# Deformable-attention bias network: four sets of 32 outputs on pairs of keys, in place of two sets of 64 on single keys

## The chip, the cores and the metric

The kernel runs on one core of one Trainium2 chip, in float32 throughout. The metric is the device time of one execution in microseconds; lower is better. A core has TensorE for matmuls (PE; its weight loads are shown apart as PEld), VectorE (DVE), ScalarE (ACT), GpSimd (POOL) and SyncE (SP), which mostly starts transfers.

## The reference, cut to what matters

Four layers follow each other: a deformable attention block with an MLP, then three smaller attention-like blocks. Only the attention of the first is touched. It has 2 batches and 8 heads of 64 channels; 1024 queries (32 x 32 pixels) look at 64 sampled keys per head. Beside the usual q·k score each (query, key) has a bias from a small network on their relative position:

```
pos  = grid_q[:, :, None, :] - grid_kv[:, None, :, :]        # 2 numbers per (query, key)
bias = sign(pos) * log1p(abs(pos))
bias = relu(bias @ cpb_w1 + cpb_b1)                          # 2 -> 128
bias = relu(bias @ cpb_w2 + cpb_b2)                          # 128 -> 128
bias = bias @ cpb_w3 + cpb_b3                                # 128 -> 1
sim  = einsum('bhid,bhjd->bhij', qh, kh) + bias
out  = softmax(sim) @ v
```

That is 2 x 8 x 64 x 1024, about a million (query, key) pairs, each through a 128 x 128 layer. The signs of `cpb_w3` decide how outputs of the second layer can be added before the third: |w3| is multiplied into the second layer's weights (a relu lets a positive factor through), so the third layer is a sum with signs +1 and -1.

## The kernel before, in words

A step treats one key of two heads (512 steps n, in 8 groups g of 64; a group is a batch and a pair of heads).

- `first(n)` (line 334): VectorE adds an x part and a y part out of a small table, with a relu: two instructions (heads) of 128 x 1024 into `h1`, 128 hidden units on the partitions. Three `h1` buffers; it runs two keys ahead.
- `second(n, o)` (line 553), o = 0 and 1: TensorE, four column tiles of 32 side by side, eight matmuls of 512 columns (each shows as two records), into PSUM tile `ph`; ScalarE evicts it with bias and relu into `r0` or `r1`. Each `r` tile has 64 hidden units of the one half of the pixels and 64 of the other on its partitions. `ph` has two buffers.
- `combine(n)` (line 571): VectorE computes r0 += rel * r1, where `rel` is the ratio of signs of the two halves, so that the third layer has a contraction over 64 for each half of the pixels.
- `third(g, i)` (line 592): on four keys, TensorE multiplies the combined tiles by a window of the sign columns `cw3` and adds into the score tile `psim`, which `scores(g)` (line 575) started with q·k. The score tile's 128 rows mix 64 keys and the two halves of the pixels.
- `attend(g, ...)` (line 714): eviction of `psim`, transposes (`flip`), maximum (`top`), `sub`, `exp`, `total`, `norm`, transposes back (`back`), spread as small pieces over the next group's steps. `prepare(g)` (line 609) computes the sampled keys and values of a coming group, spread in the same way. A convolution's taps on VectorE (`chain`, line 830) and the tables' scaling on ScalarE are spread too.

The spreading is written out by hand: `at(n, when, fn)` files a piece of work under a step and a half-step, and `run(n, when)` emits it there. `pin` keeps each engine's instructions of this part in the program's order. So an engine's order is the order in which the loop calls the functions:

```
for n in range(NK):
    second(n, 0);  run(n, 0)
    second(n, 1);  first(n + 2);  combine(n - 1);  run(n, 1)
```

Ahead of that loop stands a lead-in (lines 352 to 532): loads, normalization, queries, transposes of x and the offset convolution of the first group, with small instructions that make `sgn`, `rel`, `b2a`, `cw3` and the weights `w2a`. Behind it stand the output projection, the MLP and the other three layers.

Of the kernel before, what the change touches and what calls it, by code (L numbers as in the profile page):

```python
# [10 lines left out]
F32 = mybir.dt.float32  # L11
# [25 lines left out]
    ("L0_conv_cpb_w1", 2), ("L0_conv_cpb_b1", 1), ("L0_conv_cpb_b2", 2), ("L0_conv_cpb_w3", 2),  # L37
# [27 lines left out]
def conv_seq(  # L65
# [60 lines left out]
    with ExitStack() as ctx_l0:  # L126
# [3 lines left out]
        kblk = l0.tile([P, 2, 2, P], F32, name="kblk")  # L130
# [195 lines left out]
        w2a = l0.tile([P, P], F32, name="w2a")  # L326
        sgn = l0.tile([P, 2], F32, name="sgn")
        b2a = l0.tile([P, 2], F32, name="b2a")
        cw3 = l0.tile([P, 47], F32, name="cw3")
        rel = l0.tile([P, 1], F32, name="rel")  # L330
        h1p = ctx_att.enter_context(tc.tile_pool(name="h1p", bufs=3))
# [20 lines left out]
        with tc.tile_pool(name="a", bufs=1) as a, tc.tile_pool(name="aps", bufs=3, space=PSUM) as aps, tc.tile_pool(  # L352
# [75 lines left out]
            pin(nc.vector.tensor_scalar(sgn, v("L0_conv_cpb_w3"), 0.0, 2.0, ALU.is_ge, ALU.mult))  # L428
            pin(nc.vector.tensor_scalar(sgn, sgn, -1.0, None, ALU.add))
            pin(nc.vector.memset(cw3, 0.0))  # L430
            pin(nc.vector.tensor_copy(cw3[0:DH, 15:16], sgn[0:DH, 0:1]))
            pin(nc.vector.tensor_copy(cw3[DH:P, 31:32], sgn[DH:P, 0:1]))
            pin(nc.vector.tensor_tensor(rel, sgn[:, 0:1], sgn[:, 1:2], ALU.mult))
            pin(nc.vector.tensor_tensor(b2a, v("L0_conv_cpb_w3"), sgn, ALU.mult))
            pin(nc.vector.tensor_tensor(b2a, b2a, v("L0_conv_cpb_b2"), ALU.mult))
# [77 lines left out]
            pin(nc.scalar.activation(w2a, cpbw[:, P : 2 * P], AF.Abs))  # L513
            pin(nc.vector.tensor_tensor(w2a, w2a, cpbw[:, 0:P], ALU.mult))
# [23 lines left out]
        with tc.tile_pool(name="hid", bufs=3) as hid, tc.tile_pool(name="sm", bufs=1) as sm, tc.tile_pool(name="hps", bufs=2, space=PSUM) as hps, tc.tile_pool(  # L538
# [3 lines left out]
            r0s, r1s, psims = {}, {}, {}  # L542
# [10 lines left out]
            def second(n, o):  # L553
                ph = hps.tile([P, 2, 512], F32, name="ph")
                for h in range(2):
                    for t in range(4):
                        half, s = divmod(t, 2)
                        pin(
                            nc.tensor.matmul(  # L559
                                ph[t * 32 : (t + 1) * 32, h, :],  # L560
                                lhsT=w2a[:, o * DH + s * 32 : o * DH + (s + 1) * 32],
                                rhs=h1s[n][:, h, half * 512 : (half + 1) * 512],
                                start=True,
                                stop=True,
                            )
                        )
                r = hid.tile([P, 2, 512], F32, name=f"r{o}", bufs=(7, 3)[o])
                pin(nc.scalar.activation(r, ph, AF.Relu, bias=b2a[:, o : o + 1]))  # L568
                (r0s, r1s)[o][n] = r

            def combine(n):
                r0, r1 = (r.rearrange("p h n -> p (h n)") for r in (r0s[n], r1s.pop(n)))
                pin(nc.vector.scalar_tensor_tensor(r0, r1, rel, r0, ALU.mult, ALU.add))  # L573

            def scores(g):
                k, b = divmod(g, B)
                ps = psims[g] = sps.tile([P, 2, 512], F32, name="psim")
                for half in range(2):
                    for h in range(2):
                        hs = slice(h * DH, (h + 1) * DH)  # L580
                        pin(
                            nc.tensor.matmul(  # L582
                                ps[:, h, :],
                                lhsT=kblk[hs, g % 2, half, :],
                                rhs=q[hs, k, b * HW + half * 512 : b * HW + (half + 1) * 512],
                                start=(half == 0),
                                stop=False,
                                skip_group_check=True,
                            )
                        )  # L590

            def third(g, i):
                n = g * J + 4 * i
                for h in range(2):
                    for m in range(4):
                        pin(
                            nc.tensor.matmul(  # L597
                                psims[g][m * 32 : (m + 1) * 32, h, :],
                                lhsT=cw3[:, 15 - i : 47 - i],
                                rhs=r0s[n + m][:, h, :],  # L600
                                start=False,
                                stop=(i == 15),
                                skip_group_check=True,
                            )
                        )
                for m in range(4):
                    del r0s[n + m]

            def prepare(g):
# [53 lines left out]
                def keys():  # L663

                    for half in range(2):
                        pin(
                            nc.vector.tensor_scalar(
                                kblk[:, g % 2, half, :].rearrange("p (m s i) -> p m s i", m=4, s=2)[:, :, half, :],
                                st["pk"][:, 0, :].rearrange("p (m i) -> p m i", m=4),
                                DH**-0.5,  # L670
                                None,
                                ALU.mult,
                            )
                        )

                def values():
                    for h in range(2):
                        hs = slice(h * DH, (h + 1) * DH)
                        pin(nc.vector.tensor_copy(vblk[hs, g % 2, h, :], st["pk"][hs, 1, :]))
# [34 lines left out]
            def attend(g, n, step):  # L714
# [4 lines left out]
                def evict(h):  # L719
                    if h == 0:  # L720
# [3 lines left out]
                            st["simt"][:, h, :], psims[g][:, h, :], AF.Identity, bias=v("L0_conv_cpb_b3")  # L724
# [3 lines left out]
                def flip(h):  # L728

                    pt = st["pt", h] = mps.tile([P, 4, 2, 4, 16], F32, name="psm", tag="m")  # L730
                    for t in range(4):
                        pin(
                            nc.tensor.transpose(
                                pt[:, t].rearrange("p s m i -> p m s i"), st["simt"][:, h, t * P : (t + 1) * P], ident
# [3 lines left out]
                def top(h):  # L738
                    if h == 0:
                        st["mx"] = sm.tile([P, 2, 8], F32, name="mx")  # L740
                        st["e"] = sm.tile([P, 2, 4, 2, J], F32, name="e")
                        st["den"] = sm.tile([P, 2, 8], F32, name="den")
                    pt = st["pt", h].rearrange("p t s m i -> p (t s) (m i)")
                    pin(nc.vector.tensor_reduce(st["mx"][:, h, :], pt, AX.X, ALU.max))

                def sub(h):
                    pt = st["pt", h].rearrange("p t s m i -> p t s (m i)")
                    mx = st["mx"][:, h, :].rearrange("p (t s) -> p t s", s=2)
                    pin(
                        nc.vector.tensor_tensor(  # L750
                            st["e"][:, :, :, h, :].rearrange("p s t j -> p t s j"),
                            pt,
                            mx.unsqueeze(3).to_broadcast([P, 4, 2, J]),
# [4 lines left out]
                def ef(s):  # L758
                    return st["e"][:, s].rearrange("p t h j -> p (t h) j")

                def exp(s, half):
                    es = ef(s)[:, half * 4 : half * 4 + 4, :]
                    pin(nc.scalar.activation(es, es, AF.Exp))

                def total(s):
                    pin(nc.vector.tensor_reduce(st["den"][:, s, :], ef(s), AX.X, ALU.add))

                def norm(s):
                    den = st["den"]
                    if s == 0:  # L770
                        pin(nc.vector.reciprocal(den, den))
                    pin(
                        nc.vector.tensor_tensor(
                            ef(s), ef(s), den[:, s, :].unsqueeze(2).to_broadcast([P, 8, J]), ALU.mult
                        )
                    )

                def back(s):
                    pb = st["pb", s] = mps.tile([P, 512], F32, name="pb", tag="m")
                    for t in range(4):  # L780
# [3 lines left out]
                                st["e"][:, s, t].rearrange("p h j -> p (h j)"),  # L784
# [4 lines left out]
                def keep_(s):  # L789
# [5 lines left out]
                    (2, 1, top, 0), (4, 1, sub, 0), (6, 1, top, 1), (8, 1, sub, 1),  # L795
                    (10, 0, exp, 0, 0), (11, 0, exp, 0, 1), (12, 0, exp, 1, 0), (13, 0, exp, 1, 1),
# [25 lines left out]
            for g in range(NG):  # L822
                prepare(g)
                at(J * g + 5, 1, scores, g)
                for i in range(16):
                    at(J * g + 4 * i + 5, 1, third, g, i)
                if g < NG - 1:
                    attend(g, J * (g + 1) + 2, True)
# [24 lines left out]
            for n in range(NK):  # L853
                second(n, 0)
                run(n, 0)
                second(n, 1)
                if n + 2 < NK:
                    first(n + 2)
                if n:
                    combine(n - 1)  # L860
                h1s.pop(n)
                run(n, 1)
            combine(NK - 1)
# [674 lines left out]
def _layout(a):  # L1538
# [12 lines left out]
    for name, (at, w) in _AT.items():  # L1551
# [7 lines left out]
        elif name in ("L0_conv_cpb_b2", "L0_conv_cpb_w3"):  # L1559
            x = np.tile(x.reshape(2, DH).T, (2, 1))  # L1560
# [83 lines left out]
```

## Time and profile before

| what | us |
|---|---|
| median of 3 runs (2898.55 to 2899.06) | 2899.02 |
| the profiled execution | 2898.92 |
| its span, first to last instruction | 2897.1 |
| first second layer starts | 45.8 |
| last third layer ends | 2096.4 |
| busy in the span: PE, DVE, ACT, POOL | 2848.6, 2281.3, 1510.7, 2.0 |

A group's line in the profile names the line of the kernel, the engine and the operation, the tile written and those read, the shape, the count, then busy time and mean duration in ns, then idle time of that engine just before the instructions, and what ended most of that idle time. A timeline's line gives start, duration, engine, line, operation and count. Four matmuls on neighbouring column tiles run side by side, so their durations overlap, and it is the distance between starts that says what they cost.

### The profile page before, as it was taken

Reading aid. Unit: us, or ns where it says so; the run is one execution under the profiler, and the core shown is the slowest. Engines: PE = TensorE matmul, PEld = TensorE weight load, DVE = VectorE, ACT = ScalarE, POOL = GpSimd, SP = SyncE. Lnnn points to the kernel's source line nnn. Section 1 sums busy time; section 2 is a strip of 40 time slices with the busy share of each in tenths; the row PEclk is TensorE's granted clock in tenths of the full one; section 3 lists DMA queues with packets and bytes.
Section 4 is the critical chain, followed back from the end, with each engine's and each line's share of the span. In section 5 each row is a group of like instructions: output and inputs, shape, how many; then the busy total and the mean of one; then the engine's idle time right before and its main releaser. Section 6 shows DMA issues by size and latency. Waiting matters only on the chain.

```text
span 2897.1 us, 48614 instructions
## 1 busy us (share of the span) xinstructions
PE 2848.6 (98%) x21304; PEld 1018.9 (35%) x21304; DVE 2281.3 (79%) x2486; ACT 1510.7 (52%) x1759; POOL 2.0 (0%) x8
## 2 busy tenths in 40 slices
PE   8999999999999999999999999999999999999996
PEld 4233233333333333333333333333344444455453
DVE  6999899999999989998998998898764454523545
ACT  6666666667666666666666666666512111110244
POOL 0000000000000000000000000000000000000000
PEclk9999999999999999999999999999999999999998
DMA  3000000000000000000010001000010000010001
GB/s 113 16 16 16 17 30 16 16 16 16 16 16 26 22 16 16 16 16 16 16 41 34 16 16 45 16 16 16 14 38 15 22 29 22 1 73 1 0 1 58
DMA packets 21971, 66.41 MB, mean 23 GB/s; under 512 B 1504, under 2 KB 10848, under 8 KB 17024
## 3 DMA queue, kind: packets, MB, share of 16 engines
q1 hardware_dynamic: 21328, 62.79, 6.0%
q8 instruction: 168, 2.75, 0.4%
q10 hardware_dynamic: 432, 0.52, 0.1%
q14 instruction: 43, 0.35, 0.0%
HBM read 58.84 MB, written 4.46 MB: 22 GB/s over the span
## 4 chain that ended last, share of the span: by engine, by line
PE 96%; ACT 2%; DVE 1%; DMA 0%; issue 0%; ACTq 0%; DVEq 0%; SPq 0%
PE ph L559 61%; PE psim L597 8%; PE A L1017 4%; PE D L1017 4%; PE C L1017 4%; PE pr L1264 2%; PE B L1017 2%; PE po L952 2%; PE pg L1160 1%; PE pa L1255 1%; PE pz L1366 1%; PE pu L1194 1%; PE pscore L1337 1%; PE psim L582 1%; PE pr L1377 1%; PE pf L1304 0%
## 5 line engine op out<-in xcount | busy, mean ns | idle before, releaser
L559 PE MATMUL ph<-h,w2a 128*32 128x512 f32 x16384 | 1790.4, 593 | 1.6 <-ACT r L568 1.6
L568 ACT ACTIVATE r<-ph,b2a 128x1024 f32<-128x1024 f32 x1024 | 1142.7, 1116 | 730.5 <-PE ph L559 713.2
L339 DVE CUSTOM_DVE_ANT_1 h<-tab 128x1024 f32<-128x1024 f32 x1024 | 1205.5, 1218 | 157.5 <-PE ph L559 157.2
L559 PEld LDWEIGHTS ph<-h,w2a 128*32 128x32 f32 x16384 | 524.1, 109 | 1215.4 <-issue 842.4
L573 DVE SCALAR_TENSOR_TENSOR r<-r,rel,r 128x1024 f32<-128x1024 f32 x512 | 654.2, 1278 | 7.0 <-ACT r L568 7.0
L597 PE MATMUL psim<-r,cw 128*32 128x512 f32 x2048 | 244.4, 593 | 0.0
L163 ACT ACTIVATE tab<-tab,vec 128x256 f32<-128x256 f32 x252 | 137.3, 545 | 0.0
L597 PEld LDWEIGHTS psim<-r,cw 128*32 128x32 f32 x2048 | 65.8, 110 | 155.3 <-issue 154.2
L1057 ACT COPY u<-A 128x512 f32<-128x512 f32 x16 | 9.4, 586 | 146.8 <-PE A L1017 146.8
L1036 ACT ACTIVATE h<-h,vec 128x512 f32<-128x512 f32 x32 | 23.1, 721 | 113.6 <-DVE h L1039 113.6
L1017 PE MATMUL A<-xn,w 128*128 128x512 f32 x128 | 60.3, 593 | 0.8 <-DVE x L959 0.8
L1017 PE MATMUL C<-hT,w 128*128 128x512 f32 x128 | 60.3, 592 | 0.0
L1039 DVE TENSOR_TENSOR h<-C,u 128x512 f32<-128x512 f32 x32 | 22.1, 691 | 48.3 <-PE C L1017 48.0
L1017 PE MATMUL A<-h,w 128*128 128x512 f32 x128 | 60.1, 592 | 0.0
L952 PE MATMUL po<-q,vwo 128*128 128x512 f32 x128 | 56.1, 594 | 0.4 <-ACT r L568 0.4
L1264 PE MATMUL pr<-x,A 128*128 128x512 f32 x128 | 55.1, 592 | 0.0
L220 DVE SCALAR_TENSOR_TENSOR acc<-q,vec,acc 128x128 f32<-128x128 f32 (+3 forms) x88 | 46.3, 526 | 0.8
L1077 DVE TENSOR_TENSOR x<-D,x 128x512 f32<-128x512 f32 x32 | 22.1, 691 | 26.0 <-PE D L1017 26.0
L1077 DVE TENSOR_TENSOR x<-C,x 128x512 f32<-128x512 f32 x32 | 22.1, 691 | 24.8 <-PE C L1017 24.8
L1160 PE MATMUL pg<-xt 128*128 128x512 f32 (+3 forms) x128 | 36.4, 439 | 0.8 <-ACT xt L1158 0.6
L1017 PEld LDWEIGHTS A<-xn,w 128*128 128x128 f32 x128 | 24.2, 190 | 31.8 <-issue 30.1
L1017 PEld LDWEIGHTS A<-h,w 128*128 128x128 f32 x128 | 24.3, 190 | 30.6 <-issue 30.1
(269 smaller groups left out, 1644.0 us busy)
## 6 DMA issues: line engine op xcount, KB each, us to landing
tab<-fd SPq DMA_DIRECT2D x31, 1024.0 KB, 4.6
lw<-in_l_w_dram SPq DMA_DIRECT2D x5, 1024.0 KB
x<-in_x_dram SPq DMA_DIRECT2D x4, 1024.0 KB, 5.4
w<-in_mlp_w_dram SPq DMA_DIRECT2D x8, 512.0 KB, 3.9
w<-in_mlp_w_dram SPq DMA_DIRECT2D x16, 256.0 KB, 3.0
out_dram<-r SPq DMA_DIRECT2D x8, 512.0 KB, 2.7
xn<-in_x_dram SPq DMA_DIRECT2D x3, 1024.0 KB
xn<-in_x_dram SPq DMA_DIRECT2D x4, 256.0 KB, 5.6
```

The source lines that it names most:

```text
L163: return nc.scalar.activation(tf, tf if src is None else src[:, :, :, ax, :], AF.Identity, bias=0.0 if ax == 0 else v("L0_conv_cpb_b1"), s ...
L220: pin(nc.vector.scalar_tensor_tensor(dst, src, wt_, dst, ALU.mult, ALU.add))
L339: nc.vector._custom_dve(TENSOR_ADD_SAT, out=h1[:, h], in0=tab[:, j, h, 0, :].unsqueeze(1).to_broadcast([P, 32, 32]), in1=tab[:, j, h, 1, : ...
L559: nc.tensor.matmul(ph[t * 32 : (t + 1) * 32, h, :], lhsT=w2a[:, o * DH + s * 32 : o * DH + (s + 1) * 32], rhs=h1s[n][:, h, half * 512 : (h ...
L568: pin(nc.scalar.activation(r, ph, AF.Relu, bias=b2a[:, o : o + 1]))
L573: pin(nc.vector.scalar_tensor_tensor(r0, r1, rel, r0, ALU.mult, ALU.add))
L597: nc.tensor.matmul(psims[g][m * 32 : (m + 1) * 32, h, :], lhsT=cw3[:, 15 - i : 47 - i], rhs=r0s[n + m][:, h, :], start=False, stop=(i == 1 ...
L952: nc.tensor.matmul(po, lhsT=vwo[:, k * B + t // 2, o * P : (o + 1) * P], rhs=q[:, k, ts_], start=(k == 0), stop=(k == KC - 1),)
L1017: nc.tensor.matmul(banks[bank], lhsT=a[an][k], rhs=b_[bn_][k], start=(i < 4 and k == 0), stop=(k == n - 1), skip_group_check=True,)
L1077: nc.vector.tensor_tensor(to, t, to, ALU.add)
L1160: nc.tensor.matmul(pgs[i], lhsT=xt[:, i * P : (i + 1) * P], rhs=xt[:, i * P :], start=(t == 0), stop=(t == 7),)
L1264: nc.tensor.matmul(pr, lhsT=A[b][:, k, o * P : (o + 1) * P], rhs=x[:, k, ns], start=(k == 0), stop=(k == KC - 1),)
```

## The change

The second layer's 128 outputs are made in four sets of 32. For one set, the four column tiles hold two heads by two halves of the pixels, so a `ph` tile [...] holds one set of *two* keys. Four such sets (o = 0 to 3) of a pair of keys p are evicted to `r0` to `r3`; then

- r0 += rel0 * r1 and r2 += rel1 * r3 on VectorE (`combine(p, 0)`, `combine(p, 2)`);
- r0 += r2 by a transfer that adds (`join(p)`), issued from GpSimd's queue.

For the last addition to need no factor, the outputs are ordered so that sets 0 and 2 have the same sign in each row: `order` makes that order from the signs of `cpb_w3`, by small GpSimd operations on masks, for the biases and signs and again for the 128 x 128 weights. The third layer's contraction of 128 now covers two heads and two halves of the pixels at once; a third on four keys has one matmul per key in place of two.

The score tile becomes two tiles [...], 32 keys and four (head, half) blocks of rows. `scores` uses all 128 rows of the contraction, with keys laid out in blocks (`kblk` twice as large; filled by four ScalarE instructions in place of two on VectorE). `attend` follows: a maximum over each of two key blocks and one small maximum of the two, `sub` behind both. Pieces move by one or two steps: scores to (64g + 6, 0), thirds to (64g + 4u + 6, 1), attend by two keys. `h1` gets four buffers; `r0` to `r3` get 4, 1, 2 and 1, each for a pair of keys.

```diff
-            def second(n, o):
+            def second(p, o):
                 ph = hps.tile([P, 2, 512], F32, name="ph")
-                for h in range(2):
+                for i in range(2):
                     for t in range(4):
-                        half, s = divmod(t, 2)
+                        half, h = divmod(t, 2)
                         pin(
                             nc.tensor.matmul(
-                                ph[t * 32 : (t + 1) * 32, h, :],
-                                lhsT=w2a[:, o * DH + s * 32 : o * DH + (s + 1) * 32],
-                                rhs=h1s[n][:, h, half * 512 : (half + 1) * 512],
+                                ph[t * 32 : (t + 1) * 32, i, :],
+                                lhsT=w2a[:, o],
+                                rhs=h1s[2 * p + i][:, h, half * 512 : (half + 1) * 512],
...
-                r = hid.tile([P, 2, 512], F32, name=f"r{o}", bufs=(7, 3)[o])
-                pin(nc.scalar.activation(r, ph, AF.Relu, bias=b2a[:, o : o + 1]))
+                r = hid.tile([P, 2, 512], F32, name=f"r{o}", bufs=(4, 1, 2, 1)[o])
+                pin(nc.scalar.activation(r, ph, AF.Relu, bias=sb3[:, o, 1:2]))
...
+            def combine(p, o):
+                r0, r1 = (r.rearrange("p i n -> p (i n)") for r in (rs[p, o], rs.pop((p, o + 1))))
+                i = o // 2
+                pin(nc.vector.scalar_tensor_tensor(r0, r1, rel[:, i : i + 1], r0, ALU.mult, ALU.add))
+
+            def join(p):
+                nc.gpsimd.dma_start(rs[p, 0], rs.pop((p, 2)), accum_op=ALU.add)
...
-            def third(g, i):
-                n = g * J + 4 * i
-                for h in range(2):
-                    for m in range(4):
-                        pin(
-                            nc.tensor.matmul(
-                                psims[g][m * 32 : (m + 1) * 32, h, :],
+            def third(g, u):
+                kb, i = divmod(u, 8)
+                p = (g * J + 4 * u) // 2
+                for m in range(4):
+                    pin(
+                        nc.tensor.matmul(
+                            psims[g, kb][m * 32 : (m + 1) * 32, :],
+                            lhsT=cw3[:, 7 - i : 39 - i],
+                            rhs=rs[p + m // 2, 0][:, m % 2, :],
...
-            for n in range(NK):
-                second(n, 0)
-                run(n, 0)
-                second(n, 1)
-                if n + 2 < NK:
-                    first(n + 2)
-                if n:
-                    combine(n - 1)
-                h1s.pop(n)
-                run(n, 1)
-            combine(NK - 1)
+            for p in range(NK // 2):
+                for o in range(4):
+                    n = 2 * p + o // 2
+                    second(p, o)
+                    if o == 0 and p:
+                        combine(p - 1, 2)
+                        join(p - 1)
+                    elif o == 2:
+                        combine(p, 0)
+                    elif n + 2 < NK and o % 2:
+                        first(n + 2)
+                    run(n, o % 2)
+                for i in range(2):
+                    h1s.pop(2 * p + i)
+            combine(NK // 2 - 1, 2)
+            join(NK // 2 - 1)
```

The new function that orders the outputs, and its calls in the lead-in:

```diff
+        def order(to, of, w3, pool):
+            n = w3.shape[2]
+            gp = nc.gpsimd
+            m = pool(9 * n).rearrange("p (i n) -> p i n", n=n)
+            g, same, swap, other, keep_ = (m[:, 0:4], m[:, 4], m[:, 5], m[:, 6], m[:, 7])
+            tmp, nswap = m[:, 8], m[:, 0]
+            pin(nc.vector.tensor_scalar(g, w3, 0.0, None, ALU.is_ge))
+            for d, k in ((same, 2), (swap, 1)):
+                gp.tensor_tensor(d, g[:, 0], g[:, k], ALU.subtract)
+                gp.tensor_tensor(d, d, d, ALU.mult)
...
+            mix(0, (0, keep_), (1, other))
+            mix(1, (1, same), (2, swap), (0, other))
+            mix(2, (2, nswap), (1, swap))
+            gp.tensor_copy(to[:, 3], of[:, 3])
...
-            pin(nc.vector.tensor_tensor(rel, sgn[:, 0:1], sgn[:, 1:2], ALU.mult))
-            pin(nc.vector.tensor_tensor(b2a, v("L0_conv_cpb_w3"), sgn, ALU.mult))
...
+            order(sb3, wb, w3, part)
...
+            w2r = part(P)
+            w3r = cpbw[:, P : 2 * P]
+            pin(nc.scalar.activation(w2r, w3r, AF.Abs))
+            nc.gpsimd.tensor_tensor(w2r, w2r, cpbw[:, 0:P], ALU.mult)
+            order(w2a, w2r.rearrange("p (s o) -> p s o", s=4), w3r.rearrange("p (s o) -> p s o", s=4), part)
```

## The prediction

> **What bounds the kernel now.** I read the page's busy shares first, then the costliest groups, then the busy times of the stretch that the change rewrites, then its timeline.
>
> ```profile
> PE 2848.6 (98%) x21304; PEld 1018.9 (35%) x21304; DVE 2281.3 (79%) x2486; ACT 1510.7 (52%) x1759; POOL 2.0 (0%) x8
> ...
> L559 PE MATMUL ph<-h,w2a 128*32 128x512 f32 x16384 | 1790.4, 593 | 1.6 <-ACT r L568 1.6
> L568 ACT ACTIVATE r<-ph,b2a 128x1024 f32<-128x1024 f32 x1024 | 1142.7, 1116 | 730.5 <-PE ph L559 713.2
> L339 DVE CUSTOM_DVE_ANT_1 h<-tab 128x1024 f32<-128x1024 f32 x1024 | 1205.5, 1218 | 157.5 <-PE ph L559 157.2
> ...
> L573 DVE SCALAR_TENSOR_TENSOR r<-r,rel,r 128x1024 f32<-128x1024 f32 x512 | 654.2, 1278 | 7.0 <-ACT r L568 7.0
> L597 PE MATMUL psim<-r,cw 128*32 128x512 f32 x2048 | 244.4, 593 | 0.0
> ```
>
> The bias network is three quarters of the span, and TensorE hardly waits in it (idle ahead of L559: 1.6 us). ScalarE and VectorE wait for TensorE. The stretch from the first second layer to the last third layer, 46 to 2096 us:
>
> ```profile
> 46.00:2096.00 2050.00, 2046.77 (x18939) 625.95 (x18932) 1873.41 (x1741) 1321.84 (x1445) 0.00 (x0) 1.00 0.05 19
> ```
>
> The columns are PE, PEld, DVE, ACT, POOL. PE fills 2046.77 of 2050 us at full clock, but VectorE fills 1873. So cutting TensorE can win 177 us at most before VectorE is full, and VectorE's order begins to matter long before. Paces come from the timeline, as distances between starts (an instruction's own duration overlaps the next a little). PE, DVE and ACT:
>
> ```profile
> 1001.19 1.90 PE L597 MATMUL psim<-r,cw 128*32 128x512 f32 x16
> 1002.91 3.62 PE L559 MATMUL ph<-h,w2a 128*32 128x512 f32 x32
> ```
> ```profile
> 1000.36 1.28 DVE L573 SCALAR_TENSOR_TENSOR r<-r,rel,r 128x1024 f32<-128x1024 f32 x1
> 1001.55 2.35 DVE L339 CUSTOM_DVE_ANT_1 h<-tab 128x1024 f32<-128x1024 f32 x2
> 1003.82 1.28 DVE L573 SCALAR_TENSOR_TENSOR r<-r,rel,r 128x1024 f32<-128x1024 f32 x1
> ```
> ```profile
> 1001.45 1.12 ACT L568 ACTIVATE r<-ph,b2a 128x1024 f32<-128x1024 f32 x1 [0.60 <-PE ph L559]
> ```
> ```profile
> 2091.44 1.11 ACT L568 ACTIVATE r<-ph,b2a 128x1024 f32<-128x1024 f32 x1 [0.60 <-PE ph L559]
> ...
> 2092.59 1.28 DVE L573 SCALAR_TENSOR_TENSOR r<-r,rel,r 128x1024 f32<-128x1024 f32 x1 [2.15 <-ACT r L568]
> ```
>
> Read off: sixteen matmul records (one call of second, or one third on four keys) take 1.72 us, 0.43 us per round of four. A combine takes 1.19, a first 2.27 (both heads; its data is complete after 2.35). An eviction starts 0.26 after TensorE goes on to the next group (1001.45 against 1001.19), lasts 1.12, and a waiting combine starts 0.04 later (2092.59 against 2091.44 + 1.11). So a combine can start 1.41 us after TensorE has left the group that it needs.
>
> [...] The accumulating transfer is shown by no row here. [...] The trace has only SP's transfers, 1024 KB:
>
> ```profile
> tab<-fd SPq DMA_DIRECT2D x31, 1024.0 KB, 4.6
> ...
> x<-in_x_dram SPq DMA_DIRECT2D x4, 1024.0 KB, 5.4
> ```
>
> A join moves 512 KB [...]. [...] by these rows 4.6 to 5.4. I add about 1 [...], and take 6; ends 4 and 10. [...]
>
> **The change part by part.** "Before" is the profiled run: span 2897.1, run 2898.92 us, within 0.1 of the median 2899.02.
>
> 1. Third layer. 256 rounds (2048 records) become 128 rounds per pass: per four keys 1.72 becomes 0.86. TensorE: −128 × 0.86 = −110.
>
> 2. Scores. Before, two 64-row matmuls ran beside each other: 8 records in 1.72 us. Now 8 records use all 128 rows and come one after another, 3.44. +1.72 × 8 groups = +14.
>
> 3. Count of the rest. Second layers (4 per pair), evictions (4), combines (2) and firsts (2) are as many as before, at the same sizes. VectorE needs 2 × (1.19 + 2.27) = 6.92 per pair, TensorE 4 × 1.72 = 6.88 and 0.86 more for a third in every odd pair.
>
> 4. The order of VectorE: here the gain goes. Before, first ran two keys ahead, and a combine was waited for only by a third some keys later. Now the pinned order in pair p is combine(p−1, 2), first, combine(p, 0), first, and a second(p+1, 0) reads *both* keys of its pair. Let TensorE start an even pair at 0. combine(p−1, 2) needs the last eviction of the pair before: it starts at 1.41. Then 1.41 + 1.19 + 2.27 + 1.19 + 2.35 + 0.04 (for a release, as ACT to DVE) = 8.45 until the second first is usable (its middle combine needs an eviction done at 3.44 + 1.41 = 4.85, when VectorE is at 4.87, so no wait). TensorE wants it halfway through the next pair's opening group: 4.5 × 1.72 = 7.74. It stalls 0.71. The odd pair has a third: VectorE's second combine waits for an eviction until 8.45 + 0.86 + 1.72 + 1.41 = 12.44, its last first is usable at 16.02, and TensorE wants it at 16.19; no stall. So each two pairs lose 0.71, and 128 × 0.71 = +91. VectorE is idle in the odd pair and cannot use that, because its next combine waits for TensorE.
>
> 5. VectorE's other work. In an odd pair it falls into idle time. In the even pair, ahead of the last first, it adds to the stall: per group one cross, one sub, one total and one norm at about 0.6 (0.68 less overlap) and got 0.14, 2.54 × 7 = +18. Of 72 taps (0.38 to 0.6) a quarter falls there: 18 × 0.5 = +9. Against that, TensorE's own work in even pairs (flips 0.9, project 0.59, weigh 0.86) runs during the stall: −(0.71 + 0.59 + 0.71) × 7 = −14. Four small ACTIVATEs for the keys delay one eviction per group a little: +2; the smaller maximum, vblk's new strides and the order of exps cost nothing that anyone waits for.
>
> Sum of the stage: −110 + 14 + 91 + 18 + 9 − 14 + 2 = +10.
>
> 6. The join. From the end of combine(p−1, 2) at 2.7 to the third that reads it, after second(·, 1) of the next odd pair at 8.45 + 0.86 + 1.72 = 11.03, there are 8.3 us. A transfer of 6 us is hidden; r2's two buffers give more room than that. SP's table loads (one per eight pairs, 4.6 us) start as an even pair's last first ends, and the join beside them isn't the urgent one. Behind a waiting join on POOL stand only later joins.
>
> 7. Lead-in. 54 small POOL operations replace 8 DVE ones (9.4 − 8.23 = 1.2 us, in time that VectorE spends waiting for q), the first from about 8.5 us. A POOL memset of one column lasts 0.10 us, so 5 us in all at least; at 1 us each they would end at 62, past the first second layer at 45.8. I estimate 0.35 each[...]: done by some 33 us, hidden. [...] Cost +2; from −1 to +17.
>
> 8. Tail. Before, the last third ended 5.2 us after the last second layer (2091.2 to 2096.4). Now 1.41 + 1.28 + 6 + 0.86 = 9.5. The 4.3 more has the out-projection of the first batch beside it, which needs none of it. +3; 0 to 5.
>
> Total +15, so 2898.9 + 15 = 2914.
>
> **The rivals.**
>
> A. *TensorE stays the bound and the saving shows.* Without the stall and its followers (91 + 18 + 9 − 14) the run would be 2914 − 104 = 2810. For it: 177 us of VectorE reserve. Against it: the order is pinned, so the reserve comes where it can't be used. It is a matter of degree: every 0.1 us of stall is 13 us. Below 0.59 per two pairs the sum is on the faster side; at 0.4 it is 2874. The latencies behind 0.71 are read to about ±0.15, ±19 us.
>
> B. *The join is late.* From 8.3 us on, TensorE waits at each third; TensorE's other work (the page's smaller groups, some 61 us after the change) hides a part. At 10 us: 128 × 1.7 − 61 = +157, 3070; at 9 about +40, 2955. For it: no row shows an addition in a transfer, nor POOL's issue beside a busy VectorE. Against it: 1024 KB lands in 4.6 to 5.4.
>
> C. *Lead-in or tail at the upper ends:* +17 and +5, 2931.
>
> **How the numbers follow.** My forecast 0.57 (own range 2890 to 2940: ±19 of the stall with the ends of 7 and 8), A 0.17, B 0.19, C 0.07. About 0.2% (6 us) can be told from no change here. Faster by more: A and the lower edge of mine, 0.22. Within: 0.17 of mine and none else. Slower 0.61. The range 2865 to 2990 leaves out the strong form of A (0.08) and B with more than about 9.3 us (0.11).
>
> **What would show it.** Right: L597 halves in count and TensorE shows idle time ahead of ph released by DVE h, about 0.7 us in every second pair, near 100 us in all; VectorE waits for ACT r once per odd pair; joins land in about 6 us; stage length near 2060. Wrong: TensorE without gaps (A), or psim or r waiting for a DMA (B); the first second layer much after 46 us (C).

## The result, and the profile after

The changed kernel takes 2910.39 us (median of 5 runs, 2910.24 to 2913.67) against 2899.02: ratio 1.0042, 95% interval 1.0027 to 1.0057. It is slower by about 11 us, although TensorE was relieved of half of the third layer. The profiled execution took 2913.67 us, the longest of the five; the account below compares it with the profiled 2898.92 us of before, 14.8 us apart.

The page of the changed kernel: busy shares, groups, transfers.

```profile
PE 2858.9 (98%) x20280; PEld 1114.6 (38%) x20280; DVE 2288.0 (79%) x2473; ACT 1513.4 (52%) x1790; POOL 233.8 (8%) x318
...
L374 DVE CUSTOM_DVE_ANT_1 h<-tab 128x1024 f32<-128x1024 f32 x1024 | 1205.1, 1218 | 0.0
...
L625 DVE SCALAR_TENSOR_TENSOR r<-r,rel,r 128x1024 f32<-128x1024 f32 x512 | 655.9, 1281 | 177.3 <-ACT r L619 172.4
L628 POOL DMA_DIRECT2D r<-r x256 | 220.4, 861 | 1868.8 <-DVE r L625 1767.2
L651 PE MATMUL psim<-r,cw 128*32 128x512 f32 x1024 | 216.2, 593 | 0.8 <-DMA r<-r 0.8
...
r<-r POOLq DMA_DIRECT2D x256, 512.0 KB, 4.5
```

L651 has half of its records, so the work did go. What VectorE waits for has turned round. Before, first waited 157.2 us for TensorE to free an `h1` buffer: VectorE was ahead. Now first (L374) never waits, and the combine (L625) waits 172.4 us for ScalarE's eviction: VectorE is held by the newest result, and TensorE by VectorE. Don't be misled by PE's 98%: PE's busy time is modelled and closes over gaps. The same 16384 records of the second layer were 1790.4 us of it before and are 1954.8 now (L610). The gaps are seen in the weight loads; the table of waits of the changed kernel has (who, for whom, us in total, times, longest), and that of the kernel before, from 90 to 2080 us:

```profile
PEld ph L610 <- DVE h L374: 159.1, 240, 1.5
```
```profile
PEld ph L559 <- DVE h L339: 3.9, 13, 0.3
```

A part of each of the 240 is the ordinary spacing of weight loads (0.17 to 0.30 us between those of this stretch that wait for no other engine), so the loss is better measured at one stall. VectorE's timeline over two pairs, then the weight loads and the evictions about the stall:

```profile
1598.97 1.28 DVE L625 SCALAR_TENSOR_TENSOR r<-r,rel,r 128x1024 f32<-128x1024 f32 x1 [0.74 <-ACT r L619]
1600.17 2.35 DVE L374 CUSTOM_DVE_ANT_1 h<-tab 128x1024 f32<-128x1024 f32 x2
1602.44 1.28 DVE L625 SCALAR_TENSOR_TENSOR r<-r,rel,r 128x1024 f32<-128x1024 f32 x1
1603.63 2.35 DVE L374 CUSTOM_DVE_ANT_1 h<-tab 128x1024 f32<-128x1024 f32 x2
1605.90 1.28 DVE L625 SCALAR_TENSOR_TENSOR r<-r,rel,r 128x1024 f32<-128x1024 f32 x1
1607.10 2.35 DVE L374 CUSTOM_DVE_ANT_1 h<-tab 128x1024 f32<-128x1024 f32 x2
1610.02 1.28 DVE L625 SCALAR_TENSOR_TENSOR r<-r,rel,r 128x1024 f32<-128x1024 f32 x1 [0.57 <-ACT r L619]
...
1614.32 1.28 DVE L625 SCALAR_TENSOR_TENSOR r<-r,rel,r 128x1024 f32<-128x1024 f32 x1 [0.73 <-ACT r L619]
```
```profile
1604.91 0.22 PEld L610 LDWEIGHTS ph<-h,w2a 128*32 128x32 f32 x2 [0.33 <-DVE h L374]
1606.04 0.16 PEld L610 LDWEIGHTS ph<-h,w2a 128*32 128x32 f32 x8 [0.91 <-DVE h L374]
```
```profile
1602.97 1.11 ACT L619 ACTIVATE r<-ph,sb 128x1024 f32<-128x1024 f32 x1 [0.60 <-PE ph L610]
1604.68 1.11 ACT L619 ACTIVATE r<-ph,sb 128x1024 f32<-128x1024 f32 x1 [0.60 <-PE ph L610]
1607.16 1.11 ACT L619 ACTIVATE r<-ph,sb 128x1024 f32<-128x1024 f32 x1 [1.36 <-PE ph L610]
```

The first pair runs combine, first, combine, first without a gap from 1598.97; the second first is complete at 1603.63 + 2.35 = 1605.98, and at 1606.04 TensorE loads weights again. Evictions follow TensorE's groups: they are 1.72 apart undisturbed and 2.48 across the stall, so it costs 0.76 us. In the next pair, and at the opening of the one after it, VectorE has time to spare (0.57 and 0.73 us idle) and cannot use it. From 1598.97 to 1614.32 two pairs take 15.35 us, where TensorE has 8 x 1.72 + 0.86 = 14.6 to do. This stall is typical: from an even pair's first eviction to that of the next even pair, the trace has 127 such turns of two pairs. None is shorter than 15.3 us, and 54 take 15.35; the longer ones have small pieces of other work in them. 128 x 0.76 = 97 us.

### The profile page after: what moved, and what is told of

It reads as the page before. It is cut to its first block, busy times and chain, and to the rows that moved or that the text cites. A ratio compares the mean times of both kernels' runs of the same rounds, so it can differ in the third digit from the quotient of the medians.

```text
span 2911.9 us, 47488 instructions
## 1 busy us (share of the span) xinstructions
PE 2858.9 (98%) x20280; PEld 1114.6 (38%) x20280; DVE 2288.0 (79%) x2473; ACT 1513.4 (52%) x1790; POOL 233.8 (8%) x318
## 3 DMA queue, kind: packets, MB, share of 16 engines
q0 software_dynamic: 36864, 134.23, 24.2%
## 4 chain that ended last, share of the span: by engine, by line
issue 62%; PE 27%; POOL 7%; ACT 1%; DVE 1%; DMA 0%; POOLq 0%; ACTq 0%; DVEq 0%
POOL r L628 7%; PE A L1079 4%; PE D L1079 4%; PE C L1079 4%; PE pr L1326 2%; PE B L1079 2%; PE po L1014 2%; PE pg L1222 1%; PE pz L1428 1%; PE pa L1317 1%; PE pu L1256 1%; PE ph L610 1%; PE pscore L1399 1%; PE pr L1439 1%; PE pt L1419 0%
## 5 line engine op out<-in xcount | busy, mean ns | idle before, releaser
L610 PE MATMUL ph<-h,w2a 128*32 128x512 f32 x16384 | 1954.8, 594 | 7.2 <-DVE h L374 1.6
L619 ACT ACTIVATE r<-ph,sb 128x1024 f32<-128x1024 f32 x1024 | 1141.7, 1115 | 740.7 <-PE ph L610 724.3
L374 DVE CUSTOM_DVE_ANT_1 h<-tab 128x1024 f32<-128x1024 f32 x1024 | 1205.1, 1218 | 0.0
L610 PEld LDWEIGHTS ph<-h,w2a 128*32 128x32 f32 x16384 | 650.3, 109 | 1217.6 <-issue 753.5
L625 DVE SCALAR_TENSOR_TENSOR r<-r,rel,r 128x1024 f32<-128x1024 f32 x512 | 655.9, 1281 | 177.3 <-ACT r L619 172.4
L628 POOL DMA_DIRECT2D r<-r x256 | 220.4, 861 | 1868.8 <-DVE r L625 1767.2
L651 PE MATMUL psim<-r,cw 128*32 128x512 f32 x1024 | 216.2, 593 | 0.8 <-DMA r<-r 0.8
L651 PEld LDWEIGHTS psim<-r,cw 128*32 128x32 f32 x1024 | 54.3, 110 | 65.3 <-issue 62.9
```

Of the source, the lines that this page charges most:

```text
L374: nc.vector._custom_dve(TENSOR_ADD_SAT, out=h1[:, h], in0=tab[:, j, h, 0, :].unsqueeze(1).to_broadcast([P, 32, 32]), in1=tab[:, j, h, 1, : ...
L610: nc.tensor.matmul(ph[t * 32 : (t + 1) * 32, i, :], lhsT=w2a[:, o], rhs=h1s[2 * p + i][:, h, half * 512 : (half + 1) * 512], start=True, s ...
L619: pin(nc.scalar.activation(r, ph, AF.Relu, bias=sb3[:, o, 1:2]))
L625: pin(nc.vector.scalar_tensor_tensor(r0, r1, rel[:, i : i + 1], r0, ALU.mult, ALU.add))
L628: nc.gpsimd.dma_start(rs[p, 0], rs.pop((p, 2)), accum_op=ALU.add)
L651: nc.tensor.matmul(psims[g, kb][m * 32 : (m + 1) * 32, :], lhsT=cw3[:, 7 - i : 39 - i], rhs=rs[p + m // 2, 0][:, m % 2, :], start=False, s ...
```

## The experiments

The theory: the saving is lost in the order of VectorE's queue. Rivals: VectorE is simply full (load), or the transfer and GpSimd slow the stretch (transfer). Each run was timed beside the kernel before, whose medians in the three groups of runs were 2898.45, 2898.94 and 2899.43; differences below are to the changed kernel's 2910.4.

**Both firsts ahead of the second combine.**

```diff
                     if o == 0 and p:
                         combine(p - 1, 2)
                         join(p - 1)
-                    elif o == 2:
-                        combine(p, 0)
-                    elif n + 2 < NK and o % 2:
+                    elif n + 2 < NK and o in (1, 2):
                         first(n + 2)
+                    elif o == 3:
+                        combine(p, 0)
```

> VectorE's order in a pair becomes combine(p-1,2), first, first, combine(p,0); nothing else is changed. Theory of the order (TensorE waits 0.7 to 0.8 us in every second pair for the second first): that first is usable 1.19 us earlier, at 7.3 us against 7.74 wanted, so the stall goes: 2910 - 128 x 0.75 = 2815 us (2800 to 2835). Rival of the load (VectorE is simply full, whatever its order): within 20 us of 2910. Rival of the transfer (adding through a DMA from GpSimd slows the stretch): within 20 us of 2910 too.

Measured: 2820.9 us, 89.5 less, ratio to before 0.973 (0.9716 to 0.9745). TensorE's wait for first falls from 159.1 us to:

```profile
PEld ph L610 <- DVE h L374: 41.7, 120, 1.0
```

Same instructions on every engine, one pair of calls swapped. The rivals fall as the main cause.

**A first leads.**

```diff
-                    if o == 0 and p:
-                        combine(p - 1, 2)
-                        join(p - 1)
+                    if o == 0:
+                        if n + 2 < NK:
+                            first(n + 2)
+                        if p:
+                            combine(p - 1, 2)
+                            join(p - 1)
                     elif o == 2:
+                        if n + 2 < NK:
+                            first(n + 2)
                         combine(p, 0)
-                    elif n + 2 < NK and o % 2:
-                        first(n + 2)
```

> Order in a pair: first, combine(p-1,2), first, combine(p,0): a first runs in the 1.41 us in which the combine still waits for its eviction. Theory of the order: last first usable at about 5.8 us against 7.74 wanted, 1.9 us of reserve, which VectorE's small pieces can use too: 2808 us (2795 to 2825), a little under the run with both firsts behind the combine. The join starts 0.8 us later and still has about 7.4 us. Rivals of load and transfer: within 20 us of 2910.

Measured: 2809.4 us, ratio 0.9689 (0.9674 to 0.9703). This beats both kernels, the one before by 3.1% and the changed one by 3.5%. From its table of waits:

```profile
DVE h L374 <- PE ph L610: 35.7, 60, 1.8
...
PEld ph L610 <- DVE h L374: 4.8, 14, 0.8
```

VectorE waits for TensorE again, and hardly the other way round.

**The thirds in the other pair.** `r0` gets five buffers; to make room, `r1` and `r3` share one.

```diff
-                at(J * g + 6, 0, scores, g)
+                at(J * g + 8, 0, scores, g)
-                    at(J * g + 4 * u + 6, 1, third, g, u)
+                    at(J * g + 4 * u + 8, 1, third, g, u)
-                    attend(g, J * (g + 1) + 4, True)
+                    attend(g, J * (g + 1) + 6, True)
-                r = hid.tile([P, 2, 512], F32, name=f"r{o}", bufs=(4, 1, 2, 1)[o])
+                r = hid.tile([P, 2, 512], F32, name=("r0", "r13", "r2", "r13")[o], bufs=(5, 1, 2, 1)[o])
```

> VectorE's order stays. The thirds go two keys later, from the odd pair into the even pair, where TensorE waited; scores and attend move along by two keys; r0 gets a fifth buffer, r1 and r3 share one. Theory of the order: the third's 0.86 us run ahead of the wanted first and cover the 0.75 us of stall: 2910 - 95 = about 2820 us (2805 to 2840). Rival of the load: 2910 within 20, as VectorE has the same work. Rival of the transfer: some gain too, as the join has 7 us more; the run without a join tells these two apart.

Measured: 2912.4 us, no gain at all. The expectation was wrong. Its weight loads and PE's timeline:

```profile
1612.40 0.23 PEld L610 LDWEIGHTS ph<-h,w2a 128*32 128x32 f32 x2 [0.33 <-DVE h L374]
1613.54 0.16 PEld L610 LDWEIGHTS ph<-h,w2a 128*32 128x32 f32 x8 [0.91 <-DVE h L374]
```
```profile
1600.38 1.01 PE L651 MATMUL psim<-r,cw 128*32 128x512 f32 x4
1601.24 14.65 PE L610 MATMUL ph<-h,w2a 128*32 128x512 f32 x124
...
1615.73 1.01 PE L651 MATMUL psim<-r,cw 128*32 128x512 f32 x4
```

The same stall of 0.91 stands at the same distance ahead of a third (1613.54 and 1615.7; in the changed kernel 1606.04 and 1608.2). The stall isn't a property of even pairs: VectorE's path from a pair's start to the first that the next pair needs spans *one* pair, 8.45 us by the prediction's step 4, against TensorE's 7.74, or 8.60 if a third lies between. The pair without a third stalls, whichever it is. Moving the third moved the stall.

**No join.** The body of `join` only drops r2, so the bias lacks the half of its terms that sets 2 and 3 hold; all else runs.

```diff
             def join(p):
-                nc.gpsimd.dma_start(rs[p, 0], rs.pop((p, 2)), accum_op=ALU.add)
+                rs.pop((p, 2))
```

> The accumulating transfer is left out, so sets 2 and 3 are computed and combined but never added: the bias lacks half of its terms. Theory of the order: the transfer is hidden, only the tail has one: 2906 us (2900 to 2911). Rival of the transfer: 2880 or less. Rival of the load: as the theory.

Measured: 2910.9 us, 0.5 from the changed kernel, whose own runs lie 3.4 us apart. In this order, 256 transfers and all of POOL's work in the loop cost nothing that can be seen; not even the tail shows.

**One more VectorE instruction, in even or in odd pairs.**

```diff
                     elif o == 2:
+                        if p % 2 == 0:
+                            pin(nc.vector.tensor_tensor(idle, cst[:, 0:192], cst[:, 0:192], ALU.mult))
                         combine(p, 0)
```

The diff is that of the run with even pairs; the other has `p % 2 == 1`.

> One idle VectorE multiplication (128 x 192, a pace of about 0.27 us between the 0.20 of 128 columns and the 0.34 of 256) ahead of combine(p,0) in even pairs only, 128 of them. Theory of the order: it lies on the path to the first that TensorE waits for: 128 x 0.27 = +35 us on the changed kernel, 2945 (2935 to 2955). Rival of the load (VectorE full): the same +35 as with the same instructions in odd pairs.

> The same 128 idle multiplications ahead of combine(p,0) in odd pairs only. Theory of the order: VectorE waits about 0.6 us for an eviction there, so they cost nothing: 2910 (2908 to 2920). Rival of the load: +35, 2945.

Measured: 2941.2 us in even pairs, +30.8; 2913.8 in odd pairs, +3.4. VectorE's timeline in the even and in the odd run:

```profile
1608.41 0.35 DVE L920 TENSOR_TENSOR idle<-cst 128x192 f32<-128x192 f32 x1
1608.68 1.28 DVE L626 SCALAR_TENSOR_TENSOR r<-r,rel,r 128x1024 f32<-128x1024 f32 x1
```
```profile
1610.40 0.35 DVE L920 TENSOR_TENSOR idle<-cst 128x192 f32<-128x192 f32 x1
1611.06 1.28 DVE L626 SCALAR_TENSOR_TENSOR r<-r,rel,r 128x1024 f32<-128x1024 f32 x1 [0.30 <-ACT r L620]
```

The pace is 0.27 us. In even pairs 128 x 0.27 = 35 is nearly all paid; in odd pairs the wait for the eviction shrinks from 0.57 to 0.30 and takes the instruction in; the 3.4 us left are no more than runs of the changed kernel differ by. The load on VectorE is equal in the two.

**More work for TensorE, in pairs without or with a third.**

```diff
-                for i in range(2):
+                for i in (0, 0, 1) if o == 3 and p % 2 == 0 else range(2):
```

Here too the other run has `p % 2 == 1`.

> In even pairs, which have no third, the last second layer's first four matmuls are issued twice (same result), 128 x 0.86 = 110 us more work for TensorE. Theory of the order, as the run with shifted thirds corrected it (the stall belongs to the pair that has no third in it, since 6.88 us of TensorE stand there against a VectorE chain that needs 0.71 to 0.76 more): the repeat covers the stall and only 0.86 - 0.75 = 0.11 us per two pairs is seen, +14 us on the changed kernel, 2925 (2915 to 2935). Rival (TensorE's work sets the time): +110, 3020.

> The same repeat in odd pairs, which have a third. Theory of the order: nothing to cover there, the stall of the even pair stays: +110 us, 3020 (3010 to 3030). Rival (VectorE's load sets the time): both repeats cost the same small amount.

Measured: 3016.3 us with the repeat in odd pairs, +106, as much as the work itself; 2940.4 in even pairs, +30 for the same work. So some 76 us of it filled stalled time, but I had expected all but 14 hidden. Two undisturbed pairs of the run with the repeat in even pairs take 1620.05 − 1604.60 = 15.45 us on VectorE's timeline:

```profile
1604.60 1.28 DVE L625 SCALAR_TENSOR_TENSOR r<-r,rel,r 128x1024 f32<-128x1024 f32 x1 [0.70 <-ACT r L619]
...
1620.05 1.28 DVE L625 SCALAR_TENSOR_TENSOR r<-r,rel,r 128x1024 f32<-128x1024 f32 x1 [0.70 <-ACT r L619]
```

Against 15.35 that is the expected 0.1, 13 us. The other 17 can be found by comparing the 127 turns of the two traces one by one. In 24 of them TensorE has a small piece of its own between the even pair's start and the place of the stall: a projection of keys, a weigh, a flip or a part of the convolution. These 24 are 17 us longer than in the changed kernel, 0.7 each. The other 103, most of those with small pieces of VectorE's among them, are 11 us longer, 0.1 each on average. So in the 24 turns TensorE's own piece had already filled most of the stall, and the repeat, finding little left of it, cost most of its 0.86. The expectation had left TensorE's own pieces out.

**A late join.** On the version in which a first leads:

```diff
-                at(J * g + 6, 0, scores, g)
+                at(J * g + 5, 0, scores, g)
-                    at(J * g + 4 * u + 6, 1, third, g, u)
+                    at(J * g + 4 * u + 5, 1, third, g, u)
```

> On the order first, combine, first, combine: thirds and scores are taken to an earlier slot, the third behind second(p,3) of the pair in which its last join is issued (scores with it). The join, issued 3.6 us into the pair and landing 4.5 us later, is then wanted at 6.88. Theory: TensorE waits 1.2 us at each third, 128 times, less 25 us of its other work in those pairs: 2809 + 130 = 2940 us (2900 to 2990), and the profile names the DMA. If transfers are more than 4 us faster than their landing shows: 2810.

Measured: 2973.1 us, 164 above 2809.4. From its table of waits, and its transfers:

```profile
PEld psim L651 <- DVE h L374: 107.5, 75, 2.9
PE psim L651 <- DMA r<-r: 55.4, 93, 2.4
...
PEld psim L651 <- DVE r L625: 30.3, 22, 3.3
```
```profile
r<-r POOLq DMA_DIRECT2D x256, 512.0 KB, 4.5
```

I read all three rows of waits as the third waiting for the join. A third reads r and cw, not h. In the one that starts at 1301.79, the weight loads put down to h wait 1.39 us until 1303.30, and the matmul next to them goes on at 1303.33, released by the transfer (DMA r<-r); so I count the first row to the transfer too. The combine in the third row is what the join itself waits for (POOL's L628 waits 1761.9 us in all for L625). 164 / 128 = 1.28 us, close to the 1.2 that the expectation worked out from a landing of 4.5 us, though the expectation took 25 us off for TensorE's other work, of which the measured time shows nothing. So the rival of the late join was a real one, two of TensorE's groups of 1.72 us ahead of where the change has its thirds.

## Why the prediction was right, step by step

The forecast was 2914 for the profiled run; it took 2913.67. The mechanism was right: the third layer's saving was real, and VectorE's order lost it again. The agreement to 0.3 us is luck: repeated runs lie 3.4 us apart, their median 2910.4 is 3.6 under the forecast, and 6 us too little for the stall are made up by 3 too much for the small pieces and 3 for the tail. The parts, against their steps:

- Steps 1 and 2, −110 and +14: shown. A third takes 0.86 us for eight records of 593 ns each, four of them side by side, and L651 has 1024 records. Scores, eight records before and after, take 1.71 us more per group (3.63 from start to the next start, against 1.92).
- Step 4, the stall of 0.71 x 128 = 91: measured 0.76, 97 us. The chain of 8.45 took 1606.04 − (1598.97 − 1.41) = 8.48. Taking the combine off that chain gave 89.5 back, and letting a first lead 101, of the 104 that rival A counts for the stall and what follows from it. The step put the stall into even pairs and the third into odd ones, but didn't say that the stall would go along if the third moved; the expectation for the moved thirds missed that.
- Step 5, small pieces, +15. The stage, from first to last second layer, grew by 12.9 us (2058.3 against 2045.4, taken at the last eviction), where the sum of steps 1 to 5 said 10. Steps 1, 2 and 4 as measured make +1 of that, so 12 are left for the pieces. In a group without taps, an even pair's first eviction and that of the odd pair behind it are 7.63 us apart when nothing else runs. They are 8.22 apart with VectorE's cross, sub or total in between (+0.60 each, as assumed) and 8.13 with its norm. TensorE's pieces hide less than assumed: project shows 0.12, a flip 0.48 and weigh 0.78 of its 0.86. From these the hidden part is about 8 us in seven groups, not 14. The 24 turns that have taps and nothing else lost 3.6 us together; what the other taps cost of the +9 isn't separated.
- Step 6, the join: it lands in 4.5 us (4.5 to 8.3), not 6, and is hidden, as the run without it shows. The 6 was my estimate, from SP's loads of 1024 KB and about 1 us more that no row showed. The trace of before had a nearer row than those of 1024 KB: SP's weight loads of 512 KB landed in 3.9.
- Step 7, lead-in +2: it was +1.8 (47.65 against 45.81), for other reasons. The 0.35 us per POOL operation, the end at 33 and the +2 were my estimates: POOL's rows of before are memsets alone, 2.0 us of them. POOL's new operations ran from 8.74 to 20.6, 0.22 us apiece. The 22 taps, from 13.8 to 24.2, took 10.45 us with POOL beside them for two thirds of it, against 10.35 before: they were lengthened by no more than 0.1 us. Of the 1.8, 0.8 is the first load landing later (4.87 against 4.06), and 0.7 stands at the last transposes of the lead-in (1.90 from their start to the first second layer, against 1.19); its cause wasn't looked into.
- Step 8, tail +3: the last third ended 8.7 us after the last group of second layers was left, against 5.2, but what follows was 3.4 us shorter (797.3 against 800.7, from the last third to the end): +0.1. TensorE had the projection of the first batch beside it and waited only 0.8 us for the last join (L651's row above), so I should have counted the tail at next to nothing.

1.8 + 12.9 + 0.1 = 14.8, the distance of the profiled runs. Rival A's time, 2810, is what the version in which a first leads reaches (2809.4), and the other reordered one comes near (2820.9): its mechanism was right for a kernel that puts first ahead of the combine. Rival B was kept off by the 8.3 us of the join's distance; its +40 for a join of 9 us should by its own terms be 128 x 0.7 − 61 = +29, on which nothing rests.

## What to carry to other kernels

When work is cut from the engine that bounds a loop, write down for each engine, in the order that its queue is given, the path from what it waits for to what is waited for, over one turn of the loop: an engine with 9% idle time (VectorE here, busy for 1882 of 2064 us) can still be the one that sets the pace, if its idle time lies behind a wait. Put instructions that wait for nothing new ahead of those that wait for the newest result: here halving a layer was worth nothing until two calls were swapped, and 3% then. And to see whether an engine is full or only badly ordered, add one small instruction in two places: here the 128 instructions cost 30.8 us in the one and 3.4 in the other. An engine that is full should pay for both; that is my expectation, and no run here had one.

## What was not expected of the hardware

The joins move 134 MB through the transfer engines (24.2% of their time), and neither VectorE nor TensorE shows it: first takes 1218 ns before and after, a combine 1278 and 1281, a record of the second layer 593 and 594, though POOL spends 0.86 us on the issue of every join beside them. What shows them is SP's table loads of 1024 KB: they land in 5.6 us in place of 4.6, and in 4.7 without the joins. The four loads of x, as large, land in 6.9 in place of 5.4, and in 4.8 without the joins, but in 5.1 in the run with the late join, which has them all; so for these the cause isn't shown. No row of the table of waits names the table loads.
